# Attention and experts interleaved in rounds of six score units instead of four, with PSUM banks dealt out anew

## The chip, the cores and the metric

The kernel runs on one core of a Trainium2 chip. The metric is device time in microseconds (us), the median of several executions. TensorE (PE in the profile) multiplies, VectorE (DVE), ScalarE (ACT) and GpSimd (POOL) do the elementwise work, and SyncE (SP) issues most DMAs. [...]

## The reference

The input `x` has 2048 rows of 512. It is normalised per row to `xn`, and the output is `x + attention(xn) + experts(xn)`.

```python
# attention: 16 heads, each with two score maps of head size 16, causal, rotary q and k
a1, a2 = softmax(q1 k1'), softmax(q2 k2')
attn1, attn2 = [a1 v1, a1 v2], [a2 v1, a2 v2]                    # 2 x 16 wide
f = (rfft(attn1, time) - lambda * rfft(attn2, time)) * gaussian  # a filter along time
attn = irfft(f); attn = attn * rsqrt(mean(attn**2) + eps) * rms_weight * (1 - LAMBDA_INIT)
return attn @ Wout
# experts: 8 routed ones (512 -> 352 -> 512), the two best per row, and one shared (512 -> 704 -> 512)
y = sum over the two best of weight * (silu(x w1) * (x w3)) w2
return y + (silu(x sw1) * (x sw3)) sw2
```

All is fp32.

## The kernel before

There are three stages. The first normalises, routes the rows to experts, projects v, q and k, and does the shared expert for the first four row tiles (of 128 rows). The last, `ending`, does the filter along time, the norm and the output projection. The change lies in the one between, `middle(general)`: attention, with the remaining expert work laid into it. `middle` is built twice, for `general` true and false, and a flag picks one at run time by the size of the scores; with these inputs the second form (false) runs.

**Attention.** Two heads make a group; there are 8 groups (`NG`) and 4 chunks of 512 queries (`NQC`), taken in the order 3, 2, 1, 0 within each group: 32 turns, one object `Chunk` each. A *unit* is one head's scores of one block of 128 keys against the chunk's 512 queries, for both score maps: two matmuls of 64 x 128, side by side in the array, into a pair of PSUM banks (`ps_s`, line 752). ACT takes the exponential of the pair into `pt` (line 765), and where the block lies on the diagonal POOL sets the masked part to zero (line 770). When both heads of a block have their `pt`, `values` makes four matmuls of 128 x 32 that lie beside each other in the array (`ps_o`, line 796), and DVE adds `pt` to the running sums of the softmax (`sum`, line 806). There are 544 units in all; chunk 3 has 29 of them, chunk 0 five. At the end of a chunk, `sums` adds the running sums over the keys with small matmuls (`ps_sum`, line 818), `finish` transposes values and sums back (`ps_ot`, `ps_st`, lines 830 and 831), DVE divides (`rcp`, `o_n`, lines 833 to 838), and `put` writes the result into `vd` on POOL. POOL also does the first additions of the filter (`folded`) as groups are finished.

**Experts.** `experts()` is a generator. Each `yield` gives the time that its author counts for the step just issued. First come the shared expert's hidden products (`hidden`, `wh`, line 233; ACT and DVE make the gate, DVE multiplies, line 250) and its results (`wy`, line 270), for eleven row tiles in three groups. Then come 36 routed tiles of rows, each in three steps: `up_first` (`xh`), `up_third` (`xg`, whose product `xu` DVE makes at line 184), and a step that multiplies the previous tile down (`xy`), turns this one (`turned_back`, `ps_u`, copied by DVE into `uT`) and transposes the next tile's rows (`transposed`, `ps_x`). Weights of the next experts are fetched on SP's queue behind the products that read the old ones.

**The order.** TensorE, POOL and SP work in the order in which the Python code issues; ACT and DVE get their order from the framework's list scheduler. The loop at line 940 writes a round: two units of scores, the values of the round before, two more units, then expert steps until the share of expert work done equals the share of units issued (`work_all` is the sum of all steps). Ended chunks' `finish` stands ahead of the expert steps, their `sums` one round earlier behind them.

**PSUM.** Scores have two pairs of banks (pool `sc_ps`, line 568), values one bank, and everything else three banks (pool `f_ps`, line 570). A tile waits for the last reader of the tile that had its place before; places are taken in turn.

**Other buffers.** Six `pt`; keys single-buffered per head and block of 512, but for block 0, which has two sets, so that the next group's can be fetched a whole turn early (lines 655 to 664 and 929); two `u_last`.

## Time and profile before

| | us |
|---|---|
| median of 3 runs | 1388.21 (1382.71 to 1395.67) |
| the profiled execution | 1385.58 |
| its span, first to last instruction | 1383.9 |
| granted TensorE clock | 0.994 of full |
| first exponential of attention | 257.7 |
| last exponential of attention | 1250.6 |

| group, over the whole span | count | busy us |
|---|---|---|
| scores, PE L752 | 1280 | 213.1 |
| values, PE L796 | 2560 | 266.6 |
| sums of the softmax, DVE L806 | 576 | 639.1 |
| exponentials, ACT L765 | 544 | 534.1 |
| masks, POOL L770 | 256 | 161.7 |

Each line of the profile's groups names the line of the code, the engine, what is written and read, how often, and then the busy time, the mean of one in ns, and the idle time of the engine just before these instructions with what ended it. The chain of waits is followed back from the last instruction, so that a stretch in which it stays on one engine is a stretch in which that engine sets the pace. Matmuls that lie beside each other in the array run at the same time, so their busy times overlap; the start of the next piece in the chain is the better measure of how long a group took.

### The profile page before, as it was taken

Reading aid. Unit: us, or ns where it says so; the run is one execution under the profiler, and the core shown is the slowest. Engines: PE = TensorE matmul, PEld = TensorE weight load, DVE = VectorE, ACT = ScalarE, POOL = GpSimd, SP = SyncE. Lnnn points to the kernel's source line nnn. Section 1 sums busy time; section 2 is a strip of 40 time slices with the busy share of each in tenths; the row PEclk is TensorE's granted clock in tenths of the full one; section 3 lists DMA queues with packets and bytes.
Section 4 is the critical chain, followed back from the end, with each engine's and each line's share of the span. In section 5 each row is a group of like instructions: output and inputs, shape, how many; then the busy total and the mean of one; then the engine's idle time right before and its main releaser. Section 6 shows DMA issues by size and latency. Waiting matters only on the chain.

```text
span 1383.9 us, 20612 instructions
## 1 busy us (share of the span) xinstructions
PE 1334.2 (96%) x7472; PEld 618.9 (45%) x7472; DVE 1027.9 (74%) x1367; ACT 691.0 (50%) x821; POOL 578.2 (42%) x675
## 2 busy tenths in 40 slices
PE   7999999899999999999999999999999999999998
PEld 3444444333443444444445444544454454445543
DVE  7059881477777778778787888987788778877785
ACT  2311110365655566565666666666566656662321
POOL 0001222011301132036965765665579347532774
PEclk9999999999999999999999999999999999999999
DMA  9406662200210122244455655555655565557997
GB/s 374 167 16 186 195 208 69 87 17 18 76 48 32 37 75 70 80 150 139 173 178 162 214 185 178 177 181 183 201 170 198 189 199 180 170 167 246 193 223 165
DMA packets 74641, 206.58 MB, mean 149 GB/s; under 512 B 12013, under 2 KB 12177, under 8 KB 69153
## 3 DMA queue, kind: packets, MB, share of 16 engines
q1 hardware_dynamic: 61840, 177.62, 39.2%
q0 software_dynamic: 11168, 23.17, 8.3%
q10 hardware_dynamic: 1520, 4.36, 0.9%
q8 instruction: 62, 1.02, 0.3%
q14 instruction: 51, 0.41, 0.1%
HBM read 161.26 MB, written 43.85 MB: 148 GB/s over the span
## 4 chain that ended last, share of the span: by engine, by line
PE 65%; POOL 5%; DVE 4%; ACT 3%; DMA 3%; SPq 2%; issue 2%; ACTq 0%; DVEq 0%; POOLq 0%
PE ps_o L796 16%; PE ps_s L752 12%; PE wh L233 8%; PE xy L203 6%; PE xg L169 6%; PE xh L169 5%; PE wy L270 4%; ACT pt L765 3%; POOL pt L770 2%; PE ps_sum L818 2%; SPq L660 2%; DVE sum L806 2%; POOL res L1023 1%; PE po L1167 1%; PE ps_ot L830 1%
## 5 line engine op out<-in xcount | busy, mean ns | idle before, releaser
L806 DVE TENSOR_TENSOR sum<-sum,pt 128x1024 f32<-128x1024 f32 (+3 forms) x576 | 639.1, 1142 | 129.0 <-ACT pt L765 69.1
L765 ACT ACTIVATE pt<-ps_s 128x1024 f32<-128x1024 f32 x544 | 534.1, 1026 | 207.8 <-PE ps_s L752 164.6
L770 POOL TENSOR_SCALAR_AFFINE_SELECT pt<-pt 128x256 f32<-128x256 f32 x256 | 161.7, 655 | 322.8 <-ACT pt L765 322.1
L796 PE MATMUL ps_o<-pt,vd 128*32 128x512 f32 (+3 forms) x2560 | 266.6, 534 | 2.9 <-POOL pt L770 2.9
L752 PE MATMUL ps_s<-qS,kS 64*128 64x512 f32 (+3 forms) x1280 | 213.1, 414 | 17.0 <-ACT pt L765 15.3
L752 PEld LDWEIGHTS ps_s<-qS,kS 64*128 64x128 f32 x1280 | 100.2, 185 | 183.8 <-ACT pt L765 94.1
L233 PE MATMUL wh<-xnT,wu 128*128 128x512 f32 (+1 forms) x352 | 151.6, 579 | 0.0
L796 PEld LDWEIGHTS ps_o<-pt,vd 128*32 128x32 f32 x2560 | 67.0, 109 | 130.5 <-issue 115.2
L472 POOL DMA_INDIRECT who<-pairs,slot x32 | 33.1, 1036 | 208.2 <-DVE pairs L469 105.9
L847 POOL TENSOR_TENSOR vd<-o_n 128x128 f32<-128x128 f32 x62 | 42.5, 706 | 185.7 <-DVE o_n L838 131.2
L519 PE MATMUL ps_x<-xnT,wqk_sb 128*128 128x512 f32 x256 | 110.5, 593 | 0.0
L203 PE MATMUL xy<-wd,uT 128*128 128x512 f32 (+1 forms) x216 | 101.3, 605 | 0.0
L233 PEld LDWEIGHTS wh<-xnT,wu 128*128 128x128 f32 x352 | 65.1, 192 | 72.2 <-issue 54.9
L169 PE MATMUL xg<-wu,xT 128*128 128x352 f32 x288 | 95.6, 476 | 0.0
L169 PE MATMUL xh<-wu,xT 128*128 128x352 f32 x288 | 93.8, 469 | 0.7 <-ACT xT L162 0.7
L519 PEld LDWEIGHTS ps_x<-xnT,wqk_sb 128*128 128x128 f32 x256 | 48.5, 190 | 60.6 <-issue 60.6
L270 PE MATMUL wy<-wd,wu_t 128*128 128x512 f32 x160 | 73.6, 601 | 0.0
L169 PEld LDWEIGHTS xg<-wu,xT 128*128 128x128 f32 x288 | 53.9, 194 | 32.7 <-DVE sum L806 5.1
L212 ACT ACTIVATE y_sb<-xy,wcol 128x512 f32<-128x512 f32 x36 | 24.7, 687 | 85.8 <-PE xy L203 85.8
L169 PEld LDWEIGHTS xh<-wu,xT 128*128 128x128 f32 x288 | 51.9, 190 | 32.1 <-issue 5.8
L1023 POOL DMA_INDIRECT res<-ys,slot x32 | 55.8, 1743 | 21.5 <-DMA res<-ysh 10.4
L536 ACT CAST hi<-turned 128x1024 fp32r<-128x1024 f32 x16 | 16.7, 1045 | 93.8 <-DVE turned L534 83.1
(238 smaller groups left out, 1389.8 us busy)
## 6 DMA issues: line engine op xcount, KB each, us to landing
wu<-in_wex_dram SPq DMA_DIRECT2D x40, 1408.0 KB
wd<-in_wex_dram SPq DMA_DIRECT2D x39, 768.0 KB
kS<-parts_k SPq DMA_DIRECT2D x128, 128.0 KB
qS<-parts_q SPq DMA_DIRECT2D x256, 64.0 KB
ys<-y_sb SPq DMA_DIRECT2D x36, 256.0 KB
parts_q<-hi SPq DMA_DIRECT2D x32, 256.0 KB
parts_k<-hi SPq DMA_DIRECT2D x16, 256.0 KB
parts_k<-turned SPq DMA_DIRECT2D x16, 256.0 KB
```

Of the source, the lines that this page charges most:

```text
L169: nc.tensor.matmul(dst, xT[:, c, :], w[:, o : o + FI], start=(c == 0), stop=(c == NE - 1))
L203: nc.tensor.matmul(y, uT[:m, ic, :], w[:m, ic * E : (ic + 1) * E], start=(n == 0 and ic == 0), stop=(n == len(pairs) - 1 and ic == NF - 1),)
L233: nc.tensor.matmul(dst, w_sb[o // WUP][0][:, o % WUP : o % WUP + P], x[:, c, :], start=(c == 0), stop=(c == NE - 1))
L270: nc.tensor.matmul(y, us[i][:, t * P : (t + 1) * P], w_sb[i // NF][1][:, i % NF * E : (i % NF + 1) * E], start=(i == 0), stop=(i == SCH - 1),)
L519: nc.tensor.matmul(ps[:, i, :], wqk_sb[st, qk][:, i, c, :], xnT[:, c, cols], start=(c == 0), stop=(c == NE - 1),)
L752: nc.tensor.matmul(to, k, queries[2 * g + h, qc][r, off : off + w], start=True, stop=not general)
L765: nc.scalar.activation(pt[:, :, used], ps[:, :, used], AF.Exp, scale=SCALE)
L770: nc.gpsimd.affine_select(out=part, in_=part, pattern=[[0, 2], [1, P]], compare_op=ALU.is_ge, fill=0.0, base=0, channel_multiplier=-1,)
L796: nc.tensor.matmul(self.o[r : r + 32, off:], vd[:, kb, v0 : v0 + 32], pt[:, s, :], start=first, stop=self.ended, skip_group_check=True,)
L806: nc.vector.tensor_add(to, to, pt)
L847: eng.tensor_add(vd[:, self.qc * TQ : (self.qc + 1) * TQ, v0 : v0 + 32], self.o_n[:, :, h, 0, :], self.o_n[:, :, h, 1, :],)
L1023: nc.gpsimd.indirect_dma_start(out=came[k], out_offset=None, in_=ys, in_offset=bass.IndirectOffsetOnAxis(ap=slot[:, step - 2, order[k] : o ...
```

## The change

Scores get three pairs of banks, values keep one bank, and the pool of the rest has one. Where the rest needs a second bank, it takes a pair from the scores' pool, `two_banks()`, in turn with the units: `xg` (with the transposes of the next tile's rows in the other half), `ps_u`, every second hidden product of the shared expert, every second of its results, and a chunk's `finish` (both transposes in one pair). A round is three units, values, three units, then expert steps. The two up products of a routed tile are one step now, and the down product with `turned_back` the other. `sums` stands directly behind the values, in the round after the chunk's last values, and copies by ACT; `finish` stands behind the first expert step of that round. If fewer than two blocks of values stand between the bursts, an expert step goes there as well. Blocks of keys are taken from c=1 upwards, then c=0, then the diagonal; keys of c=0 have one set and are fetched at the start of the group's first turn, the others at the start of the turn that follows their last use. There are eight `pt` (six), one `u_last` (two), five places for the shared expert's products (six), and two `s_sb` (one).

```diff
-    u_last = [cpool.tile([P, QC], F32, name=f"u_last{i}") for i in range(2)]
+    u_last = cpool.tile([P, QC], F32, name="u_last")
...
-        def transposed(x):
-            ps = bank([P, NE, P], "ps_x")
+        def transposed(x, ps=None):
+            ps = bank([P, NE, P], "ps_x") if ps is None else ps.rearrange("p (c t) -> p c t", t=P)
...
-    def shared_expert(mp, fps, places=SCH):
+    def shared_expert(mp, fps, places=SCH - 1):
...
-                us.append(times(hidden(2 * i + 1, x), s))
+                us.append(times(hidden(2 * i + 1, x, spare and spare()[:, : x.shape[2]]), s))
...
-            kp, qp, pp = pool("k", 2), pool("q", 2), pool("prob", 5 if general else 6)
+            kp, qp, pp = pool("k", 2), pool("q", 2), pool("prob", 6 if general else 8)
             mp, ap = pool("ex", 2), pool("at", 2)
-            sps = pool("sc_ps", 2, space=PSUM)
+            sps = pool("sc_ps", 3, space=PSUM)
             vps = pool("av_ps", 1, space=PSUM)
-            fps = pool("f_ps", 3, space=PSUM)
+            fps = pool("f_ps", 1, space=PSUM)
...
+            def two_banks():
+                return sps.tile([P, 2, QC], F32, tag="sc", name="ps_e")
...
                     for t in range(t0, t1):
-                        y = result(us, t - t0, range(NF))
-                        yield 2.6
-                        stored(result(us, t - t0, range(NF, SCH), y), ysh[t], 0.5)
-                        yield 2.6
+                        y = two_banks()[:, 0, :] if t % 2 else None
+                        stored(result(us, t - t0, range(SCH), y), ysh[t], 0.5)
+                        yield 5.2
...
-                xT = transposed(xr.pop(0))
-                yield 0.5
+                following = transposed(xr.pop(0), two_banks()[:, 0, :])
                 for j in range(NR):
+                    xT = following
                     half = up_first(w_sb[j % 2][0], xT)
-                    yield 2.4
-                    u = up_third(w_sb[j % 2][0], xT, half)
+                    ps = two_banks()
+                    if j + 1 < NR:
+                        following = transposed(xr.pop(0), ps[:, 1, :])
+                    u = up_third(w_sb[j % 2][0], xT, half, ps[:, 0, :])
...
-                    yield 2.4
+                    yield 5.4 if j > 0 else 5.9
                     if j > 0:
                         down(*late)
                         fetch_down(es[j + 1], (j + 1) % 2, nc.sync)
-                    uT = turned_back(u)
+                    uT = turned_back(u, two_banks()[:, 0, :])
...
-                    if j + 1 < NR:
-                        xT = transposed(xr.pop(0))
...
-                    yield 3.7
+                    yield 3.1 if j > 0 else 0.5
...
-                    k = kp.tile([P, QC], F32R, tag=f"k{c}", name="kS", bufs=4 if c == 0 else 2)
+                    k = kp.tile([P, QC], F32R, tag=f"k{c}", name="kS", bufs=2)
...
-                    for kb in range(d + 1):
+                    for kb in [*range(TQ, d), *range(min(TQ, d)), d]:
...
-                    self.s_sb = ap.tile([P, P], F32, tag="s_sb", name="s_sb", bufs=1)
-                    nc.vector.tensor_copy(self.s_sb, ps)
+                    self.s_sb = ap.tile([P, P], F32, tag="s_sb", name="s_sb")
+                    nc.scalar.copy(self.s_sb, ps)
...
-                    po = bank([P, TQ, 4, 32], "ps_ot")
-                    psum = bank([P, P], "ps_st")
+                    ps = two_banks()
+                    po, psum = ps[:, 0, :].rearrange("p (t a d) -> p t a d", a=4, d=32), ps[:, 1, :P]
...
+            some = 2 if general else 3
...
-            for c in range(NQC):
+            for c in (1, 2, 0, 3):
                 load_keys(0, c)
-                if c == 0:
+                if c == 1:
                     load_queries(0, NQC - 1)
...
-                        if chunk.g + 1 < NG:
-                            load_keys(chunk.g + 1, (chunk.qc + 1) % NQC)
+                        if chunk.qc < NQC - 1:
+                            if chunk.g + 1 < NG:
+                                load_keys(chunk.g + 1, chunk.qc + 1)
+                        elif chunk.g > 0:
+                            load_keys(chunk.g, 0)
...
-            for i in range(0, len(stream), 4):
-                found = burst(stream[i : i + 2])
-                ended = values()
-                found += burst(stream[i + 2 : i + 4])
-                if todo:
-                    values()
+            for i in range(0, len(stream), 2 * some):
+                found = burst(stream[i : i + some])
+                n, ended = values()
+                for c in closing:
+                    c.sums()
+                if i and n < 2:
+                    work()
+                found += burst(stream[i + some : i + 2 * some])
+                while todo:
+                    ended += values()[1]
                 todo += found
...
-                closed = closing
-                for c in closing:
-                    c.finish()
-                while worked / work_all < (i + 4) / len(stream):
-                    took = next(ex, None)
-                    if took is None:
-                        break
-                    worked += took
-                closing = []
-                if ended is not None:
-                    ended.sums()
-                    closing = [ended]
+                closed, closing, turned = closing, ended, False
+                while worked / work_all < (i + 2 * some) / len(stream):
+                    work()
+                    if not turned:
+                        turned = True
+                        for c in closed:
+                            c.finish()
+                if not turned:
+                    for c in closed:
+                        c.finish()
```

`work()` takes one step of the generator and adds its time to `worked`. The number of steps of `folded` that a round allows rises by one.

## The prediction

> **What bounds the kernel now.** I read the page's busy table first, then stretches of 25 us, then the chain of waits inside one round, then the engine timelines around the places where the change makes TensorE depend on VectorE.
>
> ```profile
> span 1383.9 us, 20612 instructions
> ...
> PE 1334.2 (96%) x7472; PEld 618.9 (45%) x7472; DVE 1027.9 (74%) x1367; ACT 691.0 (50%) x821; POOL 578.2 (42%) x675
> ```
>
> TensorE (PE) is busy in 96% of the span. A share over all stages is not enough, so here are stretches from the attention stage (columns: busy us of PE, PEld, DVE, ACT, POOL, then clock, DMA share and GB/s; the last row sums 44 stretches from 205 to 1305 us).
>
> ```profile
> 405.00:430.00 25.00, 25.00 (x127) 9.26 (x126) 19.38 (x18) 16.07 (x18) 2.30 (x3) 1.00 0.00 0
> ...
> 1030.00:1055.00 25.00, 25.00 (x144) 11.05 (x143) 22.15 (x22) 18.37 (x23) 23.82 (x20) 1.00 0.71 226
> ...
> sum 1100.00, PE 1071.12 PEld 498.16 DVE 835.96 ACT 631.88 POOL 500.12; mean PE 24.34 PEld 11.32 DVE 19.00 ACT 14.36 POOL 11.37
> ```
>
> In a stretch of shared-expert work PE never rests and VectorE (DVE) is at 19.38 of 25. With the routed experts DVE is at 22.15 of 25: right behind PE. Over the whole stage PE rests 1100 - 1071 = 29 us. So PE's own time is the bound, and only what shortens its instruction stream, or makes it wait, counts. The chain inside one round (start, us, what) shows what a round is made of:
>
> ```profile
> 400.92 3.63 PE wh L233 x8
> 404.55 0.66 PE ps_s L752 x4
> 405.21 1.85 PE ps_o L796 x16
> 407.07 0.66 PE ps_s L752 x4
> ```
>
> and, later in the trace, a burst of scores that holds one unit instead of two:
>
> ```profile
> 855.33 0.50 PE ps_s L752 x2
> ```
>
> A round is scores 0.66, values 1.85, scores 0.66, work 3.63: 6.80 us. Back-to-back wh matmuls follow each other every 0.43 us (3.63 / 8, less a rest). Eight of them are 3.41, so 0.22 of the 3.63 is paid once, for leaving one kind of matmul for another. The 16 values matmuls run four abreast: 4 x 0.43 = 1.71, once-paid 0.14. [...] Sum of what is paid once in a round: 0.23 + 0.14 + 0.23 + 0.22 = **0.82 us**.
>
> **The change, part by part.**
>
> *Fewer rounds.* 544 units in fours are 136 rounds, in sixes 91. 45 rounds fewer x 0.82 = **-37 us**. Nothing else of PE's stream shrinks. If a burst of three cost 1.5 x 0.66, only values and work would save: 45 x 0.36 = 16 us. I take 37, since the one-unit row speaks for a fixed part, and keep 16 as the other end.
>
> *Sums behind values.* The 32 sums now stand behind work and ahead of scores; afterwards they follow matmuls of the same 128x32 shape. One switch goes each: nearest row the 0.14 of values, 32 x 0.14 = **-5** (0 to -7). Their copy s_sb, 0.285 on DVE x32 = 9 us, goes to ScalarE, which has room; nothing on the path.
>
> *Longer lead for masks and exponentials.* What is scored in the second burst is used about a half round plus a burst later than now. The waits of PE itself that this touches are small: 15.3 us for exponentials ahead of scores and 2.9 for masks ahead of values in the list of waits. I take half, **-8** (0 to -18).
>
> *The experts' banks.* Before, experts and closings had three banks of their own, used by nothing else. Now they have one, and every second product (xg, wh of odd number, ps_u, a closing's ps_ot and ps_st) takes a pair out of the scores' three. A burst of three needs all three. So the burst's third unit waits until DVE has read what the work left behind. Its cover is the switch and two units: 0.23 + 0.43 = 0.66 us. Behind that waiting matmul on PE stand the values, the second burst and the next work: the wait is PE's time in full. This is the cost that decides. DVE's rows:
>
> ```profile
> L806 DVE TENSOR_TENSOR sum<-sum,pt 128x1024 f32<-128x1024 f32 x384 | 483.3, 1289 | 101.1 <-ACT pt L765 69.1 <-POOL pt L770 28.9
> ...
> L184 DVE TENSOR_TENSOR xu<-xg,xtanh 128x352 f32<-128x352 f32 x36 | 18.6, 516 | 9.3 <-PE xg L169 8.8
> ```
>
> Only 8 of the 36 xu found DVE idle; the others stood behind a sum. Laid out by those rows, a round with an up step lasts 0.87 + 2.70 + 0.87 + 5.4 = 9.8 us on PE, and DVE has 6 x 1.29 + 0.51 + 0.51 = 8.8 to do: xu starts at once and ends 0.6 after xg, inside the cover. A round with a down step (xy 2.6, ps_u 0.33, switch) lasts 7.6 us, and DVE has 6 x 1.29 + 0.7 = 8.4: the uT copies start about 0.2 to 0.4 late and end 0.3 past the cover. The two rounds together are 17.2 of DVE on 17.4 of PE. So 36 x 0.3 = **+10**. The lower end is 0. The upper end is the delay in the trace of before: there xu ended on average 1.54 us after the last xg matmul, uT 1.41 after ps_u; past the cover that is 36 x 0.88 + 36 x 0.75 = 59. I stay near the lower end, because each wait gives DVE time to catch up.
>
> *Closings.* These rows are one closing on DVE now:
>
> ```profile
> 867.78 0.26 DVE L833 RECIPROCAL rcp<-ps_st 128x16 f32<-128x16 f32 x1
> 868.40 1.23 DVE L806 TENSOR_TENSOR sum<-sum,pt 128x1024 f32<-128x1024 f32 x1 [0.35 <-POOL pt L770]
> 869.54 0.38 DVE L836 TENSOR_SCALAR rcp<-rcp,neglam 128x8 f32<-128x8 f32 x1
> 869.92 1.23 DVE L806 TENSOR_TENSOR sum<-sum,pt 128x1024 f32<-128x1024 f32 x1
> 871.06 0.69 DVE L838 TENSOR_TENSOR o_n<-ps_ot,rcp 128x512 f32<-128x512 f32 x1
> ```
>
> Here sums slip in between, and o_n ends 4 us after its transposes; nobody needed the bank. Afterwards the transposes stand behind the first work step, and in about two of three closing rounds nothing but the next burst follows. If the three run back to back (0.25 + 0.27 + 0.69 + 0.1 = 1.3), the third unit waits 0.65: 21 closings x 0.65 = **+14**. If sums still slip in (3.7 us on average over the 32), it is 21 x 3.0 = 63; if work always followed, 0. I take 14: at the end of a ten-us round the sums of that round are nearly done.
>
> *Keys.* The first block read of a new pair of heads is now c=1, whose keys are fetched at the start of the 5-unit chunk just before, behind eight query DMAs on SP. Rows of SP's queue now:
>
> ```profile
> 873.04 3.58 SPq L672 DMA_DIRECT2D qS<-parts_q  x8
> ...
> 876.66 2.20 SPq L660 DMA_DIRECT2D kS<-parts_k  x4
> ```
>
> 3.6 + 2.2 us of issue and 2.3 (qS at the start of the stage) to 5.8 us (the gathered xrow) to land make 8 to 12. Five units are 7 us (start in the second burst) to 11 us. Seven such changes x 0.4 = **+3** (0 to 25, if expert weights hold the DMA rings). The block c=0, now single-buffered, is needed 16 units later: covered.
>
> *Small things.* When fewer than two blocks of values stand between the bursts, a work step goes there: one more switch, some 16 times x 0.22 = **+4** (0 to 6). The first round has no values to cover three exponentials: **+1**. On the one bank, xy then xh in one round wait for a copy of 0.69 that starts at once: in the +10. Probabilities have 8 buffers against 9 that are live at a peak; the sixth exponential waits for the second block's values, done before it: 0. SP's weight fetches keep their place behind xg and xy.
>
> Sum: -37 - 5 - 8 + 10 + 14 + 3 + 4 + 1 = **-18 us**. The profiled execution took 1385.6 (span 1383.9), so 1367.6; it lies 2.6 under the median shown. I say **1368**.
>
> [...]
>
> **The rivals.**
>
> *A. The banks cost more than the switches save (slower).* Mechanism: PE at the burst's third unit, waiting for DVE's xu, uT or o_n. For it: only 8 of 36 xu found DVE idle, and 22.15 of 25 us busy. Against it: an average of 19.0 of 25 leaves slack, and waiting heals the lag. Gains 50 less the small costs 8 leave 42 us: it decides from a mean wait of 42 / 91 = 0.46 us a round. At half of the delays of before, (59 + 63) / 2 = 61: -42 + 61 = +19, **1405**; at two thirds, +39, 1425.
>
> *B. About no change.* The burst's cost is proportional (16 for 37): -18 + 21 = +3, **1389**; or the waits come to about 0.4 a round.
>
> *C. It does more than I count.* DVE keeps up (0 for experts, 8 for closings), all 18 us of mask waits go: -37 - 5 - 18 + 8 + 5 = -47, **1338**.
>
> **How the numbers follow.** Forecast (-14 to -35): 0.36. C: 0.09. B, within 1% (14 us, about what a measurement of this kernel tells from no change): 0.25. A: 0.30. Faster is 0.36 + 0.09 = 0.45. Cases of both signs hold much, so the range takes C's 1338 and A at two thirds, 1425; the likeliest case alone is 1350 to 1372.
>
> **What would show it.** Right: rounds of some 8.9 us per six units; a burst of three at about 0.87 in the chain; 4 x 91 switches instead of 4 x 136; PE rest in the stage still near 30 to 50 us. Wrong: waits of scores (L752) for xu, uT, o_n or wu_t of more than 40 us in the list; bursts of about 1.0; scores waiting for kS at a change of heads; DVE above 92% through the routed stage, so that PE follows it.

## The result and the profile after

The changed kernel takes **1544.73 us** (median); the kernel before took 1386.44 us on the same chip (four runs, one more than in the table above). The ratio is 1.1137, with a 95% interval of 1.1078 to 1.1196: some 158 us slower, where 18 us faster was forecast, and 120 us above the upper end of the range. The profiled execution took 1544.19 us, with a span of 1542.5.

The page of the changed kernel, span and busy times of the engines:

```profile
span 1542.5 us, 20719 instructions
...
PE 1365.0 (88%) x7472; PEld 646.0 (42%) x7472; DVE 1006.5 (65%) x1337; ACT 695.9 (45%) x853; POOL 570.5 (37%) x672
```

The same 7472 matmuls keep PE busy for 1365.0 us of 1542.5, where they took 1334.2 of 1383.9. No other engine took its place: DVE's share fell from 74% to 65%. PE waits, and it also runs slower. The stretches of 25 us show both (columns as before: us, then busy us of PE, PEld, DVE, ACT, POOL, then granted clock, DMA share, GB/s; the last row sums the 50 stretches from 205 to 1455 us):

```profile
405.00:430.00 25.00, 23.41 (x145) 9.96 (x147) 19.81 (x21) 13.90 (x17) 4.67 (x4) 1.00 0.00 1
...
655.00:680.00 25.00, 16.53 (x79) 7.85 (x79) 1.14 (x3) 8.38 (x11) 12.37 (x25) 0.73 0.52 156
...
1030.00:1055.00 25.00, 22.58 (x158) 11.24 (x156) 17.87 (x21) 14.29 (x18) 15.54 (x18) 1.00 0.46 132
...
1105.00:1130.00 25.00, 14.69 (x60) 7.01 (x64) 1.04 (x2) 5.08 (x7) 0.95 (x1) 0.66 0.45 126
...
sum 1250.00, PE 1092.42 PEld 517.42 DVE 810.29 ACT 634.73 POOL 487.45; mean PE 21.85 PEld 10.35 DVE 16.21 ACT 12.69 POOL 9.75
```

There are two kinds of stretch. In the first and third PE rests 1.6 to 2.4 us of 25: the small, frequent waits. In the second and fourth PE is busy for 16.53 and 14.69 us, with a clock of 0.73 and 0.66, and DVE has next to nothing to do (1.14 and 1.04): it waits as well. Those lie where a new pair of heads begins. Over the stage PE rests 1250 - 1092 = 158 us, where it rested 29.

So the 158.6 us between the two profiled spans divide like this:

| | us | from |
|---|---|---|
| PE rests longer | +128 | (1542.5 - 1365.0) - (1383.9 - 1334.2) |
| PE is busy at half clock | +35 | half of 81.9 - 11.4 |
| the rest of PE's busy time | -4 | what is left |

The second row is my reading of the trace's clock records: in the stretches that they give as half clock (118 us after, 19 before) PE is busy for 81.9 and 11.4 us, and half of that counts as lost. Expert products that follow one another without a rest do take twice as long there (by the trace's starts one of xh every 0.59 us, 0.30 at full clock; one of xy every 0.85, 0.43 at full clock); that all matmuls do is assumed, so the row is an estimate. The third row is the one to be surprised at: the saving in switches was to take 37 us off PE's stream. I come back to it below.

What PE waits for, by the list of its waits (us in all, times, longest):

```profile
PE ps_s L756 <- DMA kS<-parts_k: 47.0, 17, 6.4
...
PE ps_s L756 <- DVE uT L195: 32.3, 18, 4.5
...
PE ps_e L168 <- ACT xT L161: 23.6, 35, 0.7
...
PEld ps_s L756 <- DMA kS<-parts_k: 21.7, 8, 4.1
...
PEld ps_s L756 <- DVE xu L183: 15.7, 28, 2.5
...
PE ps_s L756 <- ACT pt L769: 13.4, 28, 1.6
...
PE ps_s L756 <- DVE o_n L842: 6.2, 8, 0.8
...
PE ps_s L756 <- DVE xu L183: 4.7, 3, 2.1
```

Before, the only one of these in the list was the exponentials' (15.3). Three are new and large: **keys** (kS, 47.0 on PE), the copy **uT** out of the scores' pair (32.3), and the copy **xT** (23.6). The 21.7 us that PE's weight load (PEld) waits for keys are no second cost: 19.0 of them lie inside rests of PE that are already counted. Where an expectation below speaks of 69 us for keys, it adds the two; PE's own 47 are the figure to hold against.

A piece that waits for nothing is as short as forecast. The chain of waits in the shared-expert stretch:

```profile
405.49 0.89 PE ps_s L756 x3
406.38 2.72 PE ps_o L800 x24
409.10 0.87 PE ps_sum L822 x32
...
417.82 2.71 PE ps_o L800 x24
420.53 0.89 PE ps_s L756 x6
421.42 3.63 PE wh L232 x8
```

A burst of three is 0.89 us (0.87 was forecast), 24 values are 2.71 (2.70), and the sums behind values are 0.87 (1.01 to 1.08 before, so the 0.14 of a switch is gone). But few of the bursts behind expert work wait for nothing. Between a step of work and values, all 99 bursts of two took 0.66 us before, from their start to the start of the values. Of the bursts of three there, 64 ran at full clock; 12 of them took 0.89 us, and the middle one 1.23 (my reading of the trace's starts). An ordinary one:

```profile
680.17 1.24 PE L756 MATMUL ps_s<-qS,kS 64*128 64x512 f32 x6
681.34 2.78 PE L800 MATMUL ps_o<-pt,vd 128*32 128x512 f32 x24
```

It takes 1.17 us, and no rest stands beside it. The row of 1.24 us runs past the start of the next one (681.41 against 681.34), as the profile models the ends of matmuls, and the short wait shows as a busy PE. The third unit waits for DVE's xu. The list of the weight load (PEld) has 28 such waits, 15.7 us; PE's own has three, 4.7 us. By the same reading of starts, net of shown rests and of half clock, all scores of the stage take 199 us, where they took 194, although 182 bursts stand in place of 269; values take 244 us in place of 254. So the saving is there piece by piece, values keep theirs, and what the scores should have saved is taken back by waits too short to show. That fits the third row of the table, -4 in place of -37.

### The profile page after: what moved, and what is told of

Its sections match the earlier page's. It is cut to its first block, busy times and chain, and to the rows that moved or that the text cites. A ratio compares the mean times of both kernels' runs of the same rounds, so it can differ in the third digit from the quotient of the medians.

```text
span 1542.5 us, 20719 instructions
## 1 busy us (share of the span) xinstructions
PE 1365.0 (88%) x7472; PEld 646.0 (42%) x7472; DVE 1006.5 (65%) x1337; ACT 695.9 (45%) x853; POOL 570.5 (37%) x672
## 4 chain that ended last, share of the span: by engine, by line
PE 50%; DMA 11%; DVE 8%; ACT 6%; issue 6%; SPq 3%; POOL 3%; ACTq 0%; DVEq 0%; POOLq 0%
PE ps_o L800 13%; PE ps_s L756 8%; DMA kS<-parts_k 7%; PE xh L168 5%; PE ps_e L168 5%; PE wh L232 4%; PE xy L202 3%; PE ps_e L232 3%; ACT pt L769 3%; DMA wu<-in_wex_dram 3%; SPq L663 2%; DVE sum L810 2%; PE wy L269 2%; PE ps_e L269 1%; PE ps_sum L822 1%
## 5 line engine op out<-in xcount | busy, mean ns | idle before, releaser
L810 DVE TENSOR_TENSOR sum<-sum,pt 128x1024 f32<-128x1024 f32 (+3 forms) x576 | 627.4, 1130 | 144.6 <-POOL pt L774 75.1
L756 PEld LDWEIGHTS ps_s<-qS,kS 64*128 64x128 f32 x1280 | 109.6, 188 | 249.3 <-issue 119.8
L851 POOL TENSOR_TENSOR vd<-o_n 128x128 f32<-128x128 f32 x60 | 66.0, 1118 | 191.7 <-DVE o_n L842 113.9
L800 PEld LDWEIGHTS ps_o<-pt,vd 128*32 128x32 f32 x2560 | 73.7, 114 | 141.8 <-issue 129.6
L168 PE MATMUL ps_e<-wu,xT 128*128 128x352 f32 x288 | 94.7, 472 | 23.6 <-ACT xT L161 23.6
L232 PE MATMUL wh<-xnT,wu 128*128 128x512 f32 (+1 forms) x232 | 101.4, 587 | 0.0
L808 DVE COPY sum<-pt 128x1024 f32<-128x1024 f32 x64 | 44.8, 722 | 53.8 <-PE ps_sum L822 40.6
L168 PEld LDWEIGHTS ps_e<-wu,xT 128*128 128x128 f32 x288 | 51.8, 189 | 55.0 <-ACT xT L161 31.9
L232 PEld LDWEIGHTS wh<-xnT,wu 128*128 128x128 f32 x232 | 43.7, 194 | 51.6 <-issue 45.8
L202 PEld LDWEIGHTS xy<-wd,uT 128*128 128x128 f32 (+1 forms) x216 | 39.3, 195 | 53.3 <-issue 48.9
L581 POOL DMA_INDIRECT xrow<-xd,tok x36 | 49.2, 1368 | 31.3 <-PE ps_e L159 25.7
```

The costliest lines, as they stand in the source:

```text
L168: nc.tensor.matmul(dst, xT[:, c, :], w[:, o : o + FI], start=(c == 0), stop=(c == NE - 1))
L202: nc.tensor.matmul(y, uT[:m, ic, :], w[:m, ic * E : (ic + 1) * E], start=(n == 0 and ic == 0), stop=(n == len(pairs) - 1 and ic == NF - 1),)
L232: nc.tensor.matmul(dst, w_sb[o // WUP][0][:, o % WUP : o % WUP + P], x[:, c, :], start=(c == 0), stop=(c == NE - 1))
L581: nc.gpsimd.indirect_dma_start(out=x, out_offset=None, in_=xd, in_offset=bass.IndirectOffsetOnAxis(ap=tok[:, j : j + 1], axis=0),)
L756: nc.tensor.matmul(to, k, queries[2 * g + h, qc][r, off : off + w], start=True, stop=not general)
L800: nc.tensor.matmul(self.o[r : r + 32, off:], vd[:, kb, v0 : v0 + 32], pt[:, s, :], start=first, stop=self.ended, skip_group_check=True,)
```

## The experiments

Each was timed against the kernel before on the same chip; differences between experiments are differences of medians, and the intervals of the ratios are some ±0.2 to 0.6% (3 to 9 us).

### Is it the keys, or the banks?

**keys_order**: the first block read of a new pair of heads is c=2, fetched one turn earlier than c=1, so that its keys lead by 18 units and not five.

```diff
-                    for kb in [*range(TQ, d), *range(min(TQ, d)), d]:
+                    for kb in [*range(2 * TQ, d), *range(TQ, min(2 * TQ, d)), *range(min(TQ, d)), d]:
...
-            for c in (1, 2, 0, 3):
+            for c in (2, 1, 0, 3):
...
-                if c == 1:
+                if c == 2:
```

> The changed kernel, but a chunk reads its blocks of keys in the order c=2, c=1, c=0, diagonal, so that the keys needed first at a change of heads are those fetched a whole chunk earlier (18 units of lead for c=2, 13 for c=1, in place of 5). Theory 1 (late keys): of the changed kernel's 157 us of PE rest in the stage 69 are waits of scores for kS, and about two thirds of the 49 us lost at half clock follow these rests; both go, and the time is 1435 to 1460. Theory 2 (the experts' banks, the step my prediction called the one that decides): the rest of PE would be the same without late keys, since the waits move to xu and uT; then 1510 to 1540.

Measured: 1476.17 us, 1.0649 (1.0586 to 1.0712), 16 us above theory 1's range and 34 below theory 2's. Against 1544.73 that is -68.6 us, from an edit that moves no instruction of the experts and no bank. The clock rose from 0.962 to 0.982. Of the 71.8 us between the profiled spans, 51.5 are rest of PE that went, and 18 are half clock by the working above (81.9 to 46.2 us, halved). The list of PE's waits of this run has no row for kS among those of over 3 us, and the others stand as they were:

```profile
PE ps_s L756 <- DVE uT L195: 30.5, 18, 4.5
PE ps_e L168 <- ACT xT L161: 23.6, 35, 0.7
PE ps_s L756 <- ACT pt L769: 12.6, 29, 1.9
```

**before_new_keys**: the kernel before, with nothing new but the keys' order, buffers and fetch times of the changed one.

```diff
-                    k = kp.tile([P, QC], F32R, tag=f"k{c}", name="kS", bufs=4 if c == 0 else 2)
+                    k = kp.tile([P, QC], F32R, tag=f"k{c}", name="kS", bufs=2)
...
-                    for kb in range(d + 1):
+                    for kb in [*range(TQ, d), *range(min(TQ, d)), d]:
...
-                        if chunk.g + 1 < NG:
-                            load_keys(chunk.g + 1, (chunk.qc + 1) % NQC)
+                        if chunk.qc < NQC - 1:
+                            if chunk.g + 1 < NG:
+                                load_keys(chunk.g + 1, chunk.qc + 1)
+                        elif chunk.g > 0:
+                            load_keys(chunk.g, 0)
```

> The kernel before with only the change's order of keys: c=1 first, c=0 single-buffered and fetched at the start of the group. Theory 1 (late keys, whatever the rounds): five units are 8 to 10 us of lead against 16 us from issue to landing, so at seven changes of heads scores wait 4 to 8 us and the clock halves after: 1425 to 1460. Theory 2 (the keys are late only because the other waits have pushed SP's queue back): 1386 to 1400.

Measured: 1458.02 us, 1.0517 (1.0478 to 1.0557), +72 us over the 1385.78 beside it. The keys cost the same some 70 us with three banks for the experts and rounds of four as with one bank and rounds of six. Its list of waits:

```profile
PE ps_s L752 <- DMA kS<-parts_k: 41.2, 15, 4.8
...
PEld ps_s L752 <- DMA kS<-parts_k: 18.9, 7, 4.8
```

Again most of the second row (16.5 us of it) lies inside the rests of the first. Over the span PE rests 49 us longer than before, and half clock makes 17 us (46.2 to 11.4, halved): 66 of the 71 us between the profiled spans.

Where the time goes is in the changed kernel's chain of waits at a change of heads:

```profile
645.72 0.57 SPq L663
646.34 0.50 SPq L663
646.88 0.48 SPq L663
...
647.41 15.87 DMA kS<-parts_k
...
663.41 1.19 PE ps_s L756 x3
```

The last of the four key DMAs goes out at 647.4, and lands **15.87 us** later. PE's timeline over the same time:

```profile
652.29 0.50 PE L756 MATMUL ps_s<-qS,kS 64*128 64x512 f32 x1
654.11 0.50 PE L756 MATMUL ps_s<-qS,kS 64*128 64x512 f32 x1 [1.32 <-DMA kS<-parts_k]
658.16 0.76 PE L756 MATMUL ps_s<-qS,kS 64*128 64x512 f32 x1 [3.55 <-DMA kS<-parts_k]
663.41 1.19 PE L756 MATMUL ps_s<-qS,kS 64*128 64x512 f32 x3 [4.49 <-DMA kS<-parts_k]
```

The single matmuls of scores wait one after the other, each for the next key DMA to land: 11 us for what takes one.

**few_weights**: is the landing so long because of the experts' weights, which SP issues as well (1408 and 768 KB at a time)? Here the fetches of the later experts' weights are left out.

```diff
-                    fetch_up(es[j + 2], j % 2, nc.sync)
+                    if j + 2 >= NR:
+                        fetch_up(es[j + 2], j % 2, nc.sync)
...
-                        fetch_down(es[j + 1], (j + 1) % 2, nc.sync)
+                        if j + 1 >= NR:
+                            fetch_down(es[j + 1], (j + 1) % 2, nc.sync)
```

> The changed kernel without the fetches of the routed experts' weights inside the loop, but for the last ones that the following stage reads (36 tiles then compute with the two experts' weights that are there first). Theory 1 (keys are late because 1408 and 768 KB of weights are ahead of them in the same DMA rings: 15.9 us from the first key DMA's issue to the last landing): scores' waits for kS fall from 69 us to under 20, and the time to 1460 to 1490. Theory 2 (five units are too short a lead for any fetch, SP issuing twelve DMAs first): the waits stay above 45 us and the time above 1515.

Measured: 1522.00 us, 1.0972 (1.0941 to 1.1003), -23 us. The time lies in theory 2's range, the waits fit neither theory: PE's waits for kS fell from 47.0 us to

```profile
PE ps_s L758 <- DMA kS<-parts_k: 21.0, 10, 3.2
```

so more than half of the wait goes with the weights, and 21 us stay without them. In this run's chain of waits, at a change of heads while the shared expert runs and no weights are in flight, stands

```profile
503.69 12.49 DMA kS<-parts_k
```

The chain of the changed kernel has the same rows at every change of heads: 11.9 and 12.3 us at the two in the shared expert's time, and 13.1 to 16.4 at the five among the routed experts' weights. So these loads took 11.9 to 12.5 us without weights beside them, and 13.1 to 16.4 with them. A lead of five units (7 to 11 us) is too short either way; the weights make about half of what PE then waits.

### The copy that takes a pair out of turn

**xt_own_pair**: the transposes of the next tile's rows take a pair of their own, ahead of xg's, and no longer the other half of xg's pair.

```diff
-                    ps = two_banks()
                     if j + 1 < NR:
-                        following = transposed(xr.pop(0), ps[:, 1, :])
+                        following = transposed(xr.pop(0), two_banks()[:, 0, :])
+                    ps = two_banks()
```

> The changed kernel, but the transposes of the next tile's rows take a pair of banks of their own instead of the other half of the pair of xg. Theory: xg's first matmul waits for the copy xT out of the other half, because both halves count as one tile; 35 times 0.67 us = 24 us of PE rest go, so 1520. Rival: xg would wait anyway (for its own pair, or ACT is late for something else), and the time stays within 5 us of 1545, or rises because the step now takes two pairs of the three.

Measured: 1525.82 us, 1.1015 (1.0995 to 1.1035), -19 us where 24 were expected. The row that it aims at is this pair in the changed kernel's timeline of PE:

```profile
676.33 0.60 PE L159 MATMUL ps_e<-cst,xrow 128*128 128x128 f32 x4
677.61 2.63 PE L168 MATMUL ps_e<-wu,xT 128*128 128x352 f32 x8 [0.68 <-ACT xT L161]
```

The first line is the transposes of the *next* tile's rows into one bank of the pair; the second is xg of *this* tile into the other. The two share no bank and no data, and yet xg waits 0.68 us until ACT has copied the transposed rows away, 35 times, at every tile but one. The row is gone from this kernel's list. That the framework orders the halves of one tile as one I infer from the edit's effect; the wait itself is measured.

**keys_xt**: both edits together.

> The changed kernel with the block order of keys_order and the pair of its own of xt_own_pair. If the two costs are separate they add: 1476 less 19 to 24 gives 1452 to 1457. What is then left above the kernel before (some 68 us) should stand at the scores' third unit, as waits for DVE's uT, xu, o_n and for exponentials. If one cost was covering the other, the time stays above 1465.

Measured: 1451.31 us, 1.0467 (1.0424 to 1.051). The two add up: -68.6, and -24.9 for the second, which alone gave -18.9 (the medians are good to 3 to 9 us). What is left is 63 us above before, and of the three new rows only that for uT is left (32.8 us).

### The wait for uT

Now PE's longest wait is the copy of a turned-back expert tile, which frees the pair that a burst's third unit needs. In the changed kernel's timeline of all engines, where that wait is longest:

```profile
709.99 9.23 DVE L810 TENSOR_TENSOR sum<-sum,pt 128x1024 f32<-128x1024 f32 x5
710.35 2.25 POOL L867 TENSOR_TENSOR xnT<-vd 128x512 f32<-128x512 f32 x1
...
714.25 0.49 PE L192 MATMUL ps_e<-cst,xu 128*128 128x128 f32 x3
...
714.67 0.73 PE L756 MATMUL ps_s<-qS,kS 64*128 64x512 f32 x4
...
719.14 0.41 DVE L194 COPY uT<-ps_e 128x256 f32<-128x256 f32 x1
719.48 0.27 DVE L195 COPY uT<-ps_e 96x128 f32<-96x128 f32 x1
...
719.90 0.69 PE L756 MATMUL ps_s<-qS,kS 64*128 64x384 f32 x4 [4.50 <-DVE uT L195]
```

The turned tile is ready at 714.74. Two units are scored by 715.40, and the third finds its pair still full: DVE runs five sums without a break from 710.0 to 719.1, three of them after the turned tile is ready, and uT stands behind them in DVE's order. The five take 1.85 us each on average, while POOL works on the filter's first additions (`folded`); the mean of all 384 is 1.28. So there are three parts to it: a place in a list, an engine that has just got a burst's worth of sums, and a neighbour that slows it. In another place, at 1047 us of keys_order, the sums ahead of uT were themselves waiting for POOL's masks.

**keys_xt_ut** takes the place in the list away: ACT copies uT.

```diff
-            nc.vector.tensor_copy(uT[:, :2, :], ps[:, :2, :])
-            nc.vector.tensor_copy(uT[:96, 2, :], ps[:96, 2, :])
+            by = nc.scalar.copy if by_scalar else nc.vector.tensor_copy
+            by(uT[:, :2, :], ps[:, :2, :])
+            by(uT[:96, 2, :], ps[:96, 2, :])
```

> keys_xt, and the two copies of the turned-back product (uT, 0.41 and 0.27 us) are made by ScalarE instead of DVE. Theory 1 (the burst's third unit waits because uT stands behind sums in DVE's queue): the 30 us of rest for uT go, and some 5 to 10 us of half clock behind them: 1412 to 1425. Theory 2 (the pair itself is what is short: ScalarE's exponentials take the place of DVE's sums in front of uT): 1440 to 1455.

Measured: 1430.36 us, 1.0317 (1.0284 to 1.0349), -21 us against keys_xt, and between the two theories. The row for DVE's uT is gone from PE's list, and two that were 7.4 and 6.1 us in keys_xt have grown:

```profile
PE ps_s L757 <- DVE xu L183: 21.8, 11, 7.6
...
PE ps_s L757 <- DVE o_n L843: 11.1, 11, 2.1
```

With uT out of the way the third unit waits for the next things that DVE must clear from the pairs. This is a new wait in place of the removed one: 33 us of uT went, and some 19 came back. Theory 2's reason is not what is left: PE waits 2.4 us in all for uT on ACT. Over the whole span PE rests only 10 us less (112.1 to 102.4); 13 of the 21 us are half clock that went (49.9 to 23.7, halved).

**keys_xt_nofold** takes the slow neighbour away: POOL's first additions of the filter are left out for the first seven groups.

```diff
-                        folding = folded(ready.pop(0), nc.gpsimd)
+                        folding = iter(range(1, 9)) if ready.pop(0) >= 0 else None
...
-            for each in ([folding] if folding else []) + [folded(g, nc.gpsimd) for g in ready]:
-                for _ in each:
-                    pass
```

> keys_xt without GpSimd's folded additions of the first seven groups (left out: the first steps of the filter along time for 14 of 16 heads). Theory 1 (GpSimd's elementwise work beside DVE slows the sums, 1.23 to 1.9 us, and so uT and xu come late): the rest of PE at scores falls by half or more, and the time by 20 to 35 us. Theory 2 (DVE's order, not its speed): within 8 us of keys_xt.

Measured: 1428.97 us, 1.029 (1.0257 to 1.0323), -22 us. The mean of a sum fell from 1.282 to 1.233 us, which is 19 us of DVE over all 384, and the wait for uT from the first of these rows (keys_xt) to the second:

```profile
PE ps_s L756 <- DVE uT L195: 32.8, 18, 4.6
...
PE ps_s L756 <- DVE uT L195: 22.0, 19, 2.5
```

The longest went from 4.6 to 2.5, and as many waits remain. The neighbour explains the long ones, not that there are waits. So the time is in theory 1's range, but the row fell by a third and not by half. POOL's masks came somewhat sooner too (DVE's waits for them ahead of the sums of 128 x 1024: 36.9 to 31.3 us), so a part of the gain may be theirs.

### Are six units the wrong size?

The same banks, but bursts of two, as before. A burst of two leaves one of the three pairs to the experts.

```diff
-            some = 2 if general else 3
+            some = 2
```

**rounds_of_four** (on the changed kernel):

> The changed kernel with bursts of two on the three pairs, rounds of four; banks, steps and keys as changed. 45 more rounds at 0.82 us of switches bring back 37 us. Theory 1 (switches and bank waits are separate): 37 us more, less some of the 57 us of waits for uT, xu and wu_t, because one pair is now always left for the experts: 1525 to 1560, with the waits for DVE down by at least half. Theory 2 (bursts of three are not the cause of the bank waits): the waits for DVE stay and the time is 1575 to 1590. Keys are as late as in the changed kernel under both.

**keys_xt_four** (on keys_xt):

> keys_xt with bursts of two and rounds of four. It tells what rounds of six are worth under the new banks once keys and xT are out of the way. Prediction's sum (switches 37 us, which rounds of four give back; waits for DVE about 24 us less): about 13 us above keys_xt. By rounds_of_four against the changed kernel (24 us faster with fours): about 24 us below keys_xt, 1430.

**keys_xt_ut_four** (on keys_xt_ut):

> keys_xt_ut with rounds of four, beside rounds_of_five. Against keys_xt_four (1426) only uT moves to ScalarE, where 8.6 us of PE rest were left for it: 1416 to 1424. If rounds of six were worth what the prediction counted once the pair is no longer waited for, this would be the slower one by 15 us than rounds_of_five; if the pairs stay the bound, the two lie within 8 us.

| on top of | six units | four units | difference |
|---|---|---|---|
| the changed kernel | 1544.73 | 1520.42, 1.0966 (1.0947 to 1.0984) | -24 |
| keys_xt | 1451.31 | 1426.26, 1.0284 (1.0256 to 1.0313) | -25 |
| keys_xt_ut | 1430.36 | 1415.23, 1.0205 (1.0174 to 1.0235) | -15 |

In each setting, four units are better, though they have 45 more rounds to pay for. The expectations fared unevenly. rounds_of_four ended below both of its ranges: the waits for DVE fell by more than half (uT from 32.3 to 6.9 us), as its theory 1 has it, but the 37 us of switches did not come on top. keys_xt_four is as rounds_of_four had it. keys_xt_ut_four came out a little under its range, and neither of its two forecasts for rounds_of_five below held: that one is 31 us slower.

From keys_xt to keys_xt_four the profiled spans differ by 25.2 us. PE rests 25.8 us less (112.1 to 86.3), half clock is 9.3 less, and the rest of PE's busy time is only 10 more. So the 37 us of switches do not show as a sum here either. If they are paid all the same, six units must cost some 52 to 62 us that four don't, a part of it in waits too short to show. I read these from the starts of the units within a burst: what a unit comes later than 0.26 us after the one before it, summed over the stage (my reading of the trace; in a burst without a wait the second unit follows after 0.34 and the third after 0.23, so that up to 0.08 a burst in these sums is no wait; where a closing stands between work and scores, another sorting of the bursts moves these sums by up to 6 us).

| kernel | bursts behind work: number, us late | bursts behind values: number, us late |
|---|---|---|
| before | 103, 6.6 | 164, 24.1 |
| changed | 92, 89.5 | 88, 41.8 |
| keys_xt | 92, 73.7 | 88, 17.4 |
| keys_xt_four | 119, 25.1 | 136, 20.7 |
| keys_xt_ut | 92, 62.2 | 88, 18.1 |
| keys_xt_ut_four | 119, 23.1 | 136, 24.7 |
| rounds_of_five | 90, 16.5 | 106, 47.9 |

The bursts behind experts' work are the ones that suffer: 73.7 us with three units, 25.1 with two. That is 49 us, against the 37 that the prediction counted as saved. Two units fit into the pairs that the work left free; the third doesn't.

**rounds_of_five** tries to have both: two units behind the work, three behind the values, on keys_xt_ut.

```diff
-            some = 2 if general else 3
+            some, per = 2, 4 if general else 5
...
-            for i in range(0, len(stream), 2 * some):
+            for i in range(0, len(stream), per):
...
-                found += burst(stream[i + some : i + 2 * some])
+                found += burst(stream[i + some : i + per])
```

> keys_xt_ut with a burst of two behind the expert work and a burst of three behind the values: rounds of five. In keys_xt_ut the 92 bursts behind work lose 62 us between their units, those behind values 18. Theory 1 (the third unit behind work waits for the pair that the experts hold): two units find their pairs free, so 62 falls to 15 to 25, as in rounds of four; 18 more rounds cost 15 us; 1430 - 42 + 15 gives 1400 to 1412. Theory 2 (whatever unit comes next waits, since DVE is behind): 1425 to 1445.

Measured: 1446.14 us, 1.0423 (1.0387 to 1.0459): worse than six (1430.36) and than four (1415.23). The wait behind the work went as expected, 62.2 to 16.5, and it came back behind the values, 18.1 to 47.9. In its list of waits:

```profile
PE ps_s L757 <- ACT pt L770: 25.9, 50, 1.9
```

Three units behind the values follow two pairs whose exponentials ACT (1.03 us each on average in the changed kernel) is still taking; the row was 12.0 us in keys_xt_ut. So a third unit needs its pair freed by somebody in either place, and that somebody is DVE behind work and ACT behind values. The time misses theory 1, whose mechanism was right behind the work, by 34 us or more. It is 1 us over theory 2's range, but theory 2's reason, DVE, is not the row that grew. I take this as the best evidence that it is the third pair itself that is short and not where it is used; other rows grew beside it (7.3 us for the expert output's copy, 6.2 for queries), so the pair is not shown to be all of it.

No version beat the kernel before. The best, keys_xt_ut_four, is 27 us above it, and by then it has rounds of four again. Its PE waits 17.0 us for exponentials, 14.1 for keys and 10.4 for masks (15.3, none and 2.9 before), 23 us more in all. The keys are late again here, though keys_order had cleared their row; which of the loads these are was not followed up. How much of the rest is owed to the single bank, to the new order of blocks or to the sums' new place the runs don't separate.

## Why the prediction was wrong, by its own steps

**What bounds the kernel**: right for before, PE's own stream. What was drawn from it, that PE would go on without rest, failed. The stage rests 158 us, not the forecast 30 to 50, and DVE did not become the bound: 17.87 of 25 us in a stretch with routed experts, 22.15 before. The waits came with all the other engines busy for a smaller share of the span than before. A share of busy time answers whether an engine has room on average; each of the waits below is a question of order or of lead. The prediction's own signs of being wrong did show: waits for uT, o_n and xu of 43 us together, scores waiting for kS at a change of heads, and bursts of 1.0 us and more.

**Fewer rounds, -37, and sums behind values, -5**: right for each piece that waits for nothing (0.89 for 0.87, 2.71 for 2.70, 0.14 per sum gone), and not had as a sum. PE's busy time, half clock taken out, fell by 4 us. Values fell by some 10; the bursts of three between work and values took 1.23 us in the middle and not 0.87. Rival B's proportional price (1.5 x 0.66 = 0.99) is ruled out by the 0.89 of a burst without a wait, but its result, that the scores save nothing, is what the stage shows; short waits make it, and not a price for each unit. No run shows the 0.23 us that the sum counts as paid once in a burst of scores, nor the 0.43 of two units in the cover that the experts' banks were held against. What the traces show is the 0.34 and 0.23 us after which a second and a third unit follow, and 0.89 us for three units where two take 0.66. At 0.23 a unit 0.20 of the 0.66 is left; with it the same sum gives 0.76 a round, and 34 us for 45 rounds.

**Longer lead for masks and exponentials, -8**: not had. The scores' wait for exponentials went from 15.3 to 13.4 us, and that for masks (2.9) has left the list: -5. But the expert products that take a pair now wait for exponentials as well, 3.5 and 2.0 us in the list, and that takes the -5 back.

**Keys, +3 (0 to 25)**: this step failed by the most, **+68.6** by keys_order and +72 by before_new_keys. The working was sound in form: issue, landing, lead. The landing was mis-sized. I took 2.3 us from the queries at the start of the stage and 5.8 from gathered rows, and the row for keys itself was in the trace of before, in its chain of waits:

```profile
213.34 13.32 DMA kS<-parts_k
```

13.3 us from the last issue to the landing of just these transfers. Nobody in attention waits for it, so that of the lists of waits only SP's own has a row for key loads (54.9 us, 20 times). With it the same sum gives 3.6 + 2.2 + 13.3 = 19 us against a lead of 7 to 11: 8 to 12 us at each of seven changes, 56 to 84 us. PE's waits for keys are 47.0 us, 6.7 at a change, a little less than that. That the 68.6 lie in the middle is luck, since some 18 of them are half clock, which this sum doesn't count. A longer look at one row would still have moved the forecast to slower.

**The experts' banks, +10 (0 to 59)**: mis-sized, and for a reason that the timeline shows. The sum laid DVE's work end to end at its mean of 1.29 a sum, and let uT start 0.2 to 0.4 us late. In the trace it starts 1.6 us late on average: up to five sums stand ahead of it in DVE's fixed order, three or four before the five longest waits, and beside POOL one of them takes up to 2.3 us. The step with xu was to be "inside the cover"; the weight load of scores waits for it 28 times. "Each wait gives DVE time to catch up" was the failing clause: DVE does catch up while PE waits, but it works off the sums first, and PE waits for that. uT alone is 32.3 us, xu 4.7 in PE's list and 15.7 in its weight load's. The upper end of 59, from the delays of before, was nearer: three-unit bursts behind work are 83 us late more than before's two-unit bursts in the changed kernel, and 67 in keys_xt.

**A term that was not there: xT, 19 to 25 us.** The prediction priced which *bank* xg and the transposes use, and not that they are halves of one tile.

**Closings, +14 (0 to 63)**: 6.2 us of waits for o_n in PE's list. The lower half was right.

**The clock: no term at all.** I read 0.994 and took it for granted. With 0.962 it is worth some 35 us, so that every rest of PE was counted too cheaply. It has no experiment of its own, but goes with the rests: with the keys' waits gone it was 0.982, and between 0.980 and 0.989 in all that was built on that (profiled executions).

**The rivals.** A, that the banks cost more than the switches save, is right in sign and names a true mechanism, the third unit's wait for uT and xu. With keys and xT out of the way (keys_xt) the kernel takes 1451, over A's price of 1405 to 1425; some 19 us of that are half clock more than before. But the main part of the 158 us, the keys, was in no rival; it stood among the small terms. The range took A at two thirds and the keys' 25 not on top of it, which is why it ended at 1425.

The limit behind the waits for DVE's copies was not how much DVE had to do (busy for 65% of the span), but the order of its work: moving one copy to ACT gained 21 us. The 37 us were there in the pieces that wait for nothing, and lost again in those that wait.

## What to carry to other kernels

Price a transfer that is brought closer to its use by the row of that same transfer, found anywhere in the trace, even where nobody waits for it; a row for another transfer was off by six times here (2.3 against 13.3 us). When buffers are shared between two users, ask not whether the engine that frees them has time on average, but what stands ahead of the freeing instruction in its order; here up to five sums of a burst stood there, and the saving was undone. When several terms of a sum are waits of the engine that bounds the kernel, add the slower clock where the trace shows one behind such waits (here 0.962 for 0.994, some 35 us), and let the range add their upper ends. And hold a saving against the whole stage, not only against the pieces that have it at its best.

## What the runs showed of the hardware

**Half clock after short rests.** In the trace's clock records of the changed kernel TensorE runs at half clock in 21 windows, 118 us in all, of 3.41, 6.83, 10.24, 13.65 or 17.07 us: multiples of 3.41 (the last, 5.27, is cut off by the program's end). In before there are three, 19 us in all. By my reading each began after a stretch of 3.41 us in which PE had rested some 1.6 us or more (the least 1.56, 1.68, 1.78 and 1.79; in before 1.74, 2.28 and 2.56): about half of the window, and not all of it. The border isn't sharp by these records: in the changed kernel one stretch with 1.76 us of rest had no half clock behind it. Half clock ended after a stretch with at most 0.12 us of rest, but for the windows that the program's end cuts off. So the changed kernel's waits, those of 1.3 to 4.5 us for keys among them, cost more than their rest: some 35 us by the estimate above. The stretches with a clock of 0.73 and 0.66 above are these.

**Key loads.** Of the same key loads the last took 11.9 and 12.3 us (changed kernel) and 12.5 (few_weights) to land while the shared expert ran and no routed weights were in flight, 13.3 at the start of the stage (before), and 13.1 to 16.4 among the weights of the experts (changed kernel).

**VectorE beside GpSimd.** In the changed kernel a sum of 128 x 1024 takes 1.22 us, at most 1.23, where nothing runs on POOL (216 of 384), and 1.47 on average, up to 2.3, where POOL's additions run for all of it but 0.13 us at most (70). Without most of those additions (keys_xt_nofold) the average of all 384 is 1.23 us in place of 1.28 (keys_xt).

**Short waits of TensorE.** A wait of some 0.3 us for a bank did not show as rest: the burst at 680.17 us of the changed kernel took 1.17 us in place of 0.89 and has none beside it in PE's rows. In the weight load's a wait of 0.45 us for xu stands there, and the list of the weight load's waits has 28 waits for xu, 15.7 us in all, where PE's own has three.
